# Two small transfers change queues: the weights go to GpSimd's, the last bottom rows to ScalarE's

## The chip, the cores and the metric

The kernel runs on one core of a Trainium2 chip. Time is device microseconds of one execution. The profile of an execution has a *span*, from its first to its last instruction. A run's time and its span are recorded separately. A run more than 1.5% above the fastest of its kernel is called slow, the others fast. All comparisons use fast runs. An engine's *stream* is the list of instructions that it runs.

## The reference

For eight images of 32 channels and 128 x 128 pixels: a group norm with 16 groups, a 3 x 3 convolution computed by FFT (whose crop places the valid outputs in one corner of each image), a bias, and the input added back.

```python
x = x + conv(group_norm(x, 16), weight, bias)     # (8, 32, 128, 128), float32
```

## The kernel before

The input is laid out with 128 partitions (four pixel phases x 32 channels), two images in each of four pairs. All 16.8 MB are loaded up front by SyncE, in order; every image is summed (VectorE), squared and summed (ScalarE), normalized (ScalarE), convolved as four matmuls per block of rows (PE), added back (VectorE); the rows and columns outside the convolution get the bias from GpSimd. Stores follow in order.

The loads; every DMA has a semaphore (a counter that tells when it has landed), and each issuing engine has its own queue (q1 is SyncE's, q10 ScalarE's, q0 GpSimd's):

```python
loaded[0] = []
for half in range(2):
    rows = slice(half * H // 2, (half + 1) * H // 2)
    loaded[0].append((rows.stop, load(xts[0][:, rows, :], x[0, :, 0, rows, :])))   # SyncE
    if half == 0:
        weights_in = load(wb_sb, wb, by="act")                                     # ScalarE
for img in range(1, 4):
    loaded[img] = [(H, load(xts[img], x[img // 2, :, img % 2]))]
# ... two more pairs of images
```

GpSimd prepares constants, then waits for the weights and spreads them out (twelve copies, four into `bias_sb` and eight into `w_sb`), then makes a tiny DMA of its own:

```python
w_zero = put("pool", lambda e: e.memset(w_sb, 0.0), mark=True)
# ... four times: bias_sb copy (waits for weights_in), two w_sb copies
warm_ok = keep_warm(0, 1, w_ok)        # a matmul on PE that waits for the last copy
# ...
turned = put("pool", lambda e: e.dma_start(turn, wb[0:6, ...]), adds="moved")
```

The end, for the last image:

```python
moved = store(most, last[0:MOST, :], biased[B - 1][0], turned, by="pool")         # 189 KB
store(to[:, N : H - REST, :], xt[:, N : H - REST, :], biased[B - 1][0])           # 800 KB
store(rest[MOST:P, :], last[MOST:P, :], biased[B - 1][0])                         # 3 KB
add(B - 1, 0, 2)
add(B - 1, 2, NCHUNK)
stored = store(to[:, 0:N, :], xt[:, 0:N, :], biased[B - 1][1], *added[B - 1])     # 1056 KB
```

## Time and profile before

| | before |
|---|---|
| time, median of the 6 runs beside the changed kernel | 83.23 us (83.12 to 83.44) |
| profiled run: time, span | 83.26 us, 82.03 us |
| so outside the span | 1.23 us |
| bytes moved | 33.62 MB |
| busy shares | PE 81%, VectorE 61%, ScalarE 58%, GpSimd 39%, DMA 97% |

The record of the changed kernel's runs, and of every run of the experiments, has the span, to 0.1 us, so the time outside it can be had to about 0.05 us. In all 42 runs of the kernel before, beside the experiments below, on three chips, it is 1.18 to 1.29 us, 1.24 on average.

The page's first lines also count instructions (the numbers behind the x). GpSimd's DMA issues are in its number, ScalarE's are not: the trace of part 1 alone, below, has one ScalarE instruction fewer than that of before (56 to 57), and both pages say x53. The counts in this document are those of the programs, and the traces agree with them.

```profile
span 82.0 us, 686 instructions
...
PE 66.8 (81%) x222; PEld 41.3 (50%) x222; DVE 50.2 (61%) x43; ACT 47.9 (58%) x53; POOL 31.6 (39%) x43
```

### The profile page before, as it was taken

The numbers are of one execution on the slowest core, as the hardware profiler recorded it, in microseconds if no ns is written. First come the engines' busy times: TensorE is split into PE (matmuls) and PEld (weight loads), VectorE is DVE, ScalarE is ACT, GpSimd is POOL, SyncE is SP. The second block draws the span as 40 slices with busy tenths as digits, with TensorE's granted clock in tenths as the row PEclk, the third lists the DMA queues.
The fourth block names the chain that finished last, engine by engine and source line by source line (L and its number), as shares of the span: only waits on it lengthen the run. The fifth ranks groups of instructions, "written<-read, shape, count | busy, mean of one in ns | idle before, by whom it ended". The sixth has DMA issues, their size and how long they took to land.

```text
span 82.0 us, 686 instructions
## 1 busy us (share of the span) xinstructions
PE 66.8 (81%) x222; PEld 41.3 (50%) x222; DVE 50.2 (61%) x43; ACT 47.9 (58%) x53; POOL 31.6 (39%) x43
## 2 busy tenths in 40 slices
PE   0009974999999999999999999999999999993000
PEld 0005433566666666666666656666666666660000
DVE  0009936960899499769949995996899324006000
ACT  3307967981699299569947974994798260000000
POOL 6876000004069900106992930490085029400000
PEclk9999998579999999999999999999999999999965
DMA  2899999999979979979959889989979999999995
GB/s 40 299 415 443 463 415 423 447 407 423 551 304 511 479 320 479 511 336 431 511 256 511 383 383 511 447 352 479 463 336 423 423 431 439 431 423 419 397 430 239
DMA packets 2164, 33.62 MB, mean 410 GB/s; under 512 B 296, under 2 KB 330, under 8 KB 500
## 3 DMA queue, kind: packets, MB, share of 16 engines
q1 hardware_dynamic: 2020, 33.36, 96.3%
q0 software_dynamic: 96, 0.19, 0.6%
q10 hardware_dynamic: 48, 0.06, 0.3%
HBM read 16.84 MB, written 16.78 MB: 410 GB/s over the span
## 4 chain that ended last, share of the span: by engine, by line
PE 74%; DMA 14%; DVE 2%; SPq 1%; issue 0%
PE ps L412 73%; DMA x<-x_dram 14%; DVE x L428 2%; PE ps_m L318 1%; SPq L183 1%; PE ps_w L265 0%
## 5 line engine op out<-in xcount | busy, mean ns | idle before, releaser
L412 PE MATMUL ps<-g,w_sb 128*128 128x363 f32 (+1 forms) x192 | 60.7, 473 | 0.1
L412 PEld LDWEIGHTS ps<-g,w_sb 128*128 128x128 f32 x192 | 36.1, 194 | 20.0 <-ACT origin L292 1.4
L283 DVE TENSOR_REDUCE sums<-x 128x1 f32<-128x4096 f32 x7 | 30.9, 4411 | 0.6 <-DMA x<-x_dram 0.6
L394 POOL TENSOR_SCALAR x<-x,bias_sb 128x1984 f32<-128x1984 f32 (+3 forms) x12 | 23.2, 1945 | 18.9 <-ACT origin L292 14.6
L303 ACT ACTIVATE unused<-x,origin 128x4096 f32<-128x4096 f32 (+1 forms) x9 | 30.0, 3330 | 0.3
L428 DVE SCALAR_TENSOR_TENSOR x<-ps,bias_sb,x 128x1089 f32<-128x1089 f32 (+2 forms) x9 | 10.9, 1220 | 7.7 <-PE ps L412 7.7
L373 ACT ACTIVATE g<-x,rstd 128x1089 f32<-128x1089 f32 (+2 forms) x8 | 9.4, 1190 | 3.4 <-DVE rstd L347 3.4
L283 DVE TENSOR_REDUCE first_sums<-x 128x1 f32<-128x2048 f32 x2 | 4.6, 2286 | 6.2 <-DMA x<-x_dram 6.2
L258 POOL COPY sums<-x 128x1 f32<-128x1 f32 x6 | 1.0, 186 | 18.2 <-DMA x<-x_dram 18.2
L335 DVE TENSOR_SCALAR var<-ps_m,square 128x1 f32<-128x1 f32 x8 | 1.8, 219 | 8.2 <-ACT square L330 8.2
L265 PE MATMUL ps_w<-x,avg 128*128 128x1 f32 x4 | 0.9, 304 | 7.1 <-POOL w_sb L476 6.1
L330 ACT ACTIVATE square<-ps_m,origin 128x1 f32<-128x1 f32 x8 | 2.1, 261 | 7.3 <-PE ps_m L318 7.3
L447 PE MATMUL ps<-x,avg 128*128 128x512 f32 x6 | 4.9, 942 | 0.0
L265 PEld LDWEIGHTS ps_w<-x,avg 128*128 128x128 f32 x4 | 0.8, 248 | 7.9 <-POOL w_sb L476 6.1
L318 PEld LDWEIGHTS ps_m<-sums,avg 128*128 128x128 f32 x16 | 2.8, 188 | 2.2 <-DVE x L428 1.0
L341 ACT ACTIVATE std<-var,eps 128x1 f32<-128x1 f32 x8 | 2.4, 294 | 2.3 <-DVE var L335 2.3
L344 DVE RECIPROCAL rstd<-std 128x1 f32<-128x1 f32 x8 | 1.3, 164 | 2.9 <-ACT std L341 2.9
L292 ACT ACTIVATE origin<-ps_w 128x1 f32<-128x1 f32 x2 | 0.3, 160 | 4.0 <-PE ps_w L265 4.0
L476 POOL COPY w_sb<-wb_sb 32x128 f32<-32x128 f32 (+1 forms) x8 | 2.5, 340 | 0.0
L318 PE MATMUL ps_m<-sums,avg 128*128 128x3 f32 x16 | 2.3, 214 | 0.0
L447 PEld LDWEIGHTS ps<-x,avg 128*128 128x128 f32 x6 | 1.5, 287 | 1.0 <-issue 1.0
L237 ACT ACT_TABLE_LOAD x1 | 1.3, 1283 | 1.2 <-PEq L579 1.2
(21 smaller groups left out, 13.3 us busy)
## 6 DMA issues: line engine op xcount, KB each, us to landing
x<-x_dram SPq DMA_DIRECT2D x2, 4096.0 KB, 34.3
out_dram<-x SPq DMA_DIRECT2D x2, 4096.0 KB
x<-x_dram SPq DMA_DIRECT2D x3, 2048.0 KB, 16.0
out_dram<-x SPq DMA_DIRECT2D x3, 2048.0 KB
x<-x_dram SPq DMA_DIRECT2D x2, 1024.0 KB, 6.2
out_dram<-x SPq DMA_DIRECT2D x1, 1056.0 KB
out_dram<-x SPq DMA_DIRECT2D x1, 800.0 KB
out_dram<-x POOLq DMA_DIRECT2D x1, 189.0 KB, 7.7
```

Of the source, the lines that this page charges most:

```text
L283: lambda e: e.tensor_reduce(to_sum(img, k)[:, 0:1], piece, mybir.AxisListType.X, ALU.add),
L303: lambda e: e.activation(unused[:, rows.start * W : rows.stop * W], piece, AF.Square, bias=origins[img], accum_out=to_sum(img, k)[:, 1:2],),
L318: lambda e: e.matmul(ps_ms[:, 0 : of.shape[1]], avg, of, start=(part == 0), stop=(part == last)),
L330: lambda e: e.activation(squares[img], ps_ms[:, 0:1], AF.Square, bias=origins[img]),
L335: lambda e: e.tensor_scalar(variances[img], ps_ms[:, 1:2], squares[img], None, op0=ALU.subtract),
L341: lambda e: e.activation(stds[img], variances[img], AF.Sqrt, bias=eps, scale=float(FFT * FFT)),
L373: lambda e: e.activation(g[:, rows, :], xt[:, LO + rows.start : LO + rows.stop, LO:W], AF.Identity, bias=rstd[:, 1:2], scale=rstd[:, 0:1],),
L394: put("pool", lambda e: e.tensor_scalar(part, part, 1.0, bias_sb, op0=ALU.mult, op1=ALU.add), *free, mark=mark)
L412: lambda e, k=k, dc=dc, rows=rows, top=top: e.matmul(ps[:, 0:rows, 0 : N - dc], w_sb[:, k * P : (k + 1) * P], g[:, top : top + rows, dc:N] ...
L428: lambda e: e.scalar_tensor_tensor(part, in0=ps, scalar=bias_sb, in1=part, op0=ALU.add, op1=ALU.add),
L447: "pe", lambda e: e.matmul(pss[1][:, 0, :], avg, piece, start=True, stop=True),
L476: lambda e: e.tensor_copy(w5[to, :, dc, :, c.start * C : c.stop * C], taps[:, 1 - rin : 5 - rin, b, :].rearrange("p (dr r) b o -> p dr r ( ...
```

## The change

Its apparent intent: take the weights off ScalarE at the start, and let the bottom rows of the last image leave beside image 6's store instead of behind it.

```diff
+    put.semaphore("moved")
+    weights_in = put("pool", lambda e: e.dma_start(wb_sb, wb), adds="moved")
     loaded[0] = []
     for half in range(2):
         ...
-        if half == 0:
-            weights_in = load(wb_sb, wb, by="act")
...
-    put.semaphore("moved")
...
-    store(to[:, N : H - REST, :], xt[:, N : H - REST, :], biased[B - 1][0])
+    store(to[:, N : H - REST, :], xt[:, N : H - REST, :], biased[B - 1][0], by="act")
```

## The prediction

> **What bounds the kernel now.** I read the chain of waits first, and distrusted it; then the DMA rows of the page, because 33.62 MB in 82 us is near what this core's engines can move.
>
> ```profile
> PE 74%; DMA 14%; DVE 2%; SPq 1%; issue 0%
> ...
> DMA  2899999999979979979959889989979999999995
> ...
> q1 hardware_dynamic: 2020, 33.36, 96.3%
> q0 software_dynamic: 96, 0.19, 0.6%
> q10 hardware_dynamic: 48, 0.06, 0.3%
> HBM read 16.84 MB, written 16.78 MB: 410 GB/s over the span
> ```
>
> The chain puts 74% on PE, but it stops at 76.1 us (the last add on DVE), six microseconds before the end. The queue shares add to 97.2% of the 16 engines' span: 79.7 us of 82.0. In the packet records of the trace the first packet starts at 1.84 us and the last ends at 81.62 us, 79.8 us in all. So there is hardly a moment without a packet on each engine. The table by stretches says the same with rates:
>
> ```profile
> 2.00:4.00 2.00, 0.00 (x0) 0.00 (x0) 0.00 (x0) 0.73 (x2) 1.84 (x4) 1.00 0.85 290
> 4.00:14.00 10.00, 6.29 (x15) 3.28 (x16) 5.81 (x6) 6.03 (x9) 3.01 (x13) 0.99 1.03 435
> ...
> 70.00:76.00 6.00, 4.54 (x17) 2.68 (x15) 1.42 (x2) 0.00 (x0) 0.72 (x2) 1.00 0.99 424
> 76.00:80.00 4.00, 0.00 (x0) 0.00 (x0) 0.06 (x1) 0.00 (x0) 0.00 (x0) 0.84 0.98 411
> 80.00:82.00 2.00, 0.00 (x0) 0.00 (x0) 0.00 (x0) 0.00 (x0) 0.00 (x0) 0.50 0.57 241
> ```
>
> The last two columns are the DMA share and GB/s: 0.96 or more in every stretch from 4 to 80 us, at 411 to 435 GB/s except around 41 us, where loads give way to stores (350 in 40:43). The stores queue behind one another all the way from there: the 4 MB store of the first pair is issued at 34.37 us and lands at 52.7, the next at 49.06 and lands at 62.4, then 56.41 to 67.4, 63.74 to 72.1, 68.58 to 77.6 (issue times and landings of the semaphores, from the trace). No store is issued late enough to leave the engines without work. The last one shows how much room is left:
>
> ```profile
> SPq L552 <- DMA out_dram<-x: 4.2, 1, 4.2
> ...
> 74.58 1.48 DVE x L428 x2
> ```
>
> DVE is done at 76.06; the last store (1056 KB) is issued at 76.09; its first packet starts only at 77.98, because packets of the bottom rows (800 KB, issued at 69.01) still run until 79.09. A DMA on free engines went from issue to first packet in 1.03 us (x, 0.81 to 1.84). So the last store could have come 77.98 - 76.09 - 1.03 = 0.86 us later without harm. PE, DVE and ACT have that much slack at the end; the bound is the total work of the 16 DMA engines.
>
> **What the Trainium skill says.**
> - "DMA: Bandwidth & Descriptors", section "Issuing engines are not separate DMA queues": DMAs issued by ScalarE, SyncE or GpSimd run on the same 16 engines and interleave, and several issuers save only sequencer time. The trace agrees: the weights' packets on q10 sit between x packets of q1, and while GpSimd's store runs (74.7 to 77.2 us) q1 slows by what q0 takes.
> - Same page, "Specifications": a fabric ceiling of 435 GB/s. The stretch 4:14 reads 435, so the stream is at it, and another queue can't raise it.
> - Same page, "Latency and other measured facts": first byte after about 600 ns on the hardware path, about 1 us on GpSimd's. Here the hardware path took 1.03 us, and GpSimd's two DMAs took 4.4 us (19.03 to 23.40) and 4.7 us (70.03 to 74.71), both with the engines full. The measurement decides: GpSimd's path is far slower than stated when q1 has a backlog.
> - Same page, "Why a DMA increments its semaphore by 16 and not by 1": how many engines share a DMA follows from the outer sizes, and a GpSimd DMA on fewer than 16 starts at a moving cursor. The weights have 32 rows, so 16 engines with two packets each: the trace has 32 packets of 1984 B. I expect that this leaves the cursor, and so the placing of GpSimd's store on 14 engines (42 packets of 4608 B in the trace), as it was; no run here shows it.
>
> **Part 1: the weights move from ScalarE's queue to GpSimd's.**
>
> ```profile
> 0.81 0.41 ACTq L183 DMA_DIRECT2D wb_sb<-wb_dram  x1
> ...
> 3.09 0.45 POOL L229 TENSOR_TENSOR avg<-half 128x128 f32<-128x128 f32 x1
> ...
> 4.46 0.18 POOL L472 COPY bias_sb<-wb_sb 32x1 f32<-32x1 f32 x1 [0.46 <-DMA wb_sb<-wb_dram]
> ...
> 7.00 0.63 POOL L476 COPY w_sb<-wb_sb 32x256 f32<-32x256 f32 x2
> ...
> 11.28 1.10 PE L447 MATMUL ps<-x,avg 128*128 128x512 f32 x2
> 13.39 0.38 PE L265 MATMUL ps_w<-x,avg 128*128 128x1 f32 x2 [1.00 <-DMA x<-x_dram]
> ```
>
> Removed: 0.41 us of issue on ScalarE, which has nothing to do then but its table load. Added: one issue ahead of GpSimd's chain. Its DMA at 19.03 took 0.74 us after 0.48 us of idle that the profile puts down to issue: about 1.2 us. That moves avg from 3.54 to about 4.8 us; the first matmul wants it when the first half image lands, at 5.97. Hidden, 1.2 us to spare.
>
> The landing: before, 4.41 us. After, the descriptors come at about 2 us, just as q1 fills. With the full 4.4 us to the first packet it would be 5.2, and then a second packet and a completion, each behind one x packet of 0.31 us (their duration at that stage), plus about 0.4 us to land: 6.7 us at worst. With less backlog, about 5. My estimate is 5.5, so 1.1 us later. The twelve copies from 4.46 to 7.63 us then end at about 8.7 (9.9 at worst). The first consumer on PE is the warming matmul at 11.28, and it can itself slip until 12.3 (13.39 less 1.10), as the next matmul waits for image 1, which lands at 13.34. So the slack is 3.6 to 4.7 us against 1.1 to 2.3 us of delay. Hidden as well.
>
> What DMA work changes? The same 32 packets of 81 ns (0.16 us per engine) and 16 completions go over another queue. Image 1's landing has the same bytes ahead of it either way. Net 0, perhaps a tenth either way in the ramp of the first two microseconds (290 GB/s).
>
> **Part 2: the bottom rows move from SyncE's queue to ScalarE's.** It removes one issue of 0.95 us from SyncE, which at that time has 5 us to wait for the last add anyway. ScalarE's last activation ends at 66.9 us, so it can issue at 69.0, as SyncE did. The 128 packets of 6400 B (0.244 us each, 8 per engine, 1.95 us per engine) no longer stand behind image 6's 2 MB but alternate with them: the bottom rows land earlier or at the same time, image 6 later, both finished by about 79.1 as before, since each engine has the same packets to do. The last store stays on q1, and its 8 packets of 0.319 us per engine follow: 79.1 + 2.55 gives 81.6, and 0.34 us to land gives 81.96, as now. When two queues mixed in the trace (76.5 to 77.0), the packets' summed rate was 417 instead of 431 GB/s: over six microseconds 14/431 would be 0.2 us, but those packets were smaller, so I count 0 to 0.1 us.
>
> **Sum:** 0 (GpSimd's issue) + 0 (weights later) + 0 to 0.1 (mixing) - 0 to 0.1 (a freer ramp, SyncE free earlier) = 0 on 83.19 us. I put it at 83.15.
>
> **The rivals.**
> - *The weights become the bound at the start.* For it: GpSimd's DMAs took 6.6 and 7.7 us from issue to landing. Against it: even a landing at 8.5 us ends the copies at 11.7, before 12.3, and then the end has 0.86 us more slack. The time moves only by what exceeds about 10.0 us of landing. If that comes: 83.5 to 84.
> - *Two queues fill the engines better.* For it: the ramp and the tail (80:82 at 0.57) are not full, and the engines' last landings spread from 80.86 to 81.96. Against it: 411 to 435 GB/s everywhere else, and each engine's sum of packets stays. If it holds: 82.7 to 82.9.
> - *The placing of GpSimd's store turns.* A cursor moved by the weights would put its 13.8 KB per engine (three packets of 0.178 us, 0.53 us) on other engines; if the last one gets them: 83.5. If a late one loses them: 82.9.
>
> **Range and chances.** Runs of one kernel spread by 0.14 us (83.12 to 83.26); the rivals reach 0.3 to 0.4 us to either side. So 82.8 to 83.5. A change of 2% is 1.66 us; nothing above comes near it: 0.01 faster, 0.98 same, 0.01 slower.
>
> **What would show it.** Right: the DMA shares still add to about 97%, with first packet at 1.8 and last end near 81.6; GpSimd's first copy starts at 5 to 6.7 us; image 1's matmul still waits for its landing at about 13.3; bottom rows' packets lie among image 6's, which lands near 79; the last landing is near 82. Wrong: the warming matmul waiting for the weight copies past 12.3 us, a DMA row with a gap before the last store, or last landings of the engines spread by much more than 1.1 us.

## The result and the profile after

The changed kernel took 83.96 us (median of 6 runs, 83.46 to 84.08), the kernel before 83.23. A ratio here is the mean time of one kernel's fast runs over that of the other's fast runs of the same rounds, so it isn't quite the ratio of the medians: 1.0076, 95% interval 1.0048 to 1.0104. It is slower by 0.6 to 0.7 us, well inside the 2% within which two times count as the same here, but outside the predicted range (82.8 to 83.5).

The span does not show where. First the page of the changed kernel:

```profile
span 82.0 us, 686 instructions
...
PE 67.0 (82%) x222; PEld 41.2 (50%) x222; DVE 50.2 (61%) x43; ACT 48.0 (59%) x53; POOL 32.1 (39%) x44
...
DMA  2899999998979979959969889989979999999995
...
q1 hardware_dynamic: 1876, 32.54, 94.0%
q10 hardware_dynamic: 144, 0.82, 2.4%
q0 software_dynamic: 128, 0.26, 0.8%
```

The span is 82.0 us, as before; the queue shares still add to 97.2%. The table by stretches (its last two columns: DMA share, GB/s) differs from that of before, in these two columns and from 4 us on, by 6% at most:

```profile
4.00:14.00 10.00, 7.42 (x15) 3.75 (x15) 5.75 (x6) 6.01 (x9) 4.20 (x15) 1.00 1.04 430
...
70.00:76.00 6.00, 3.61 (x14) 2.11 (x12) 1.48 (x2) 0.00 (x0) 0.00 (x0) 1.00 1.00 427
76.00:80.00 4.00, 0.00 (x0) 0.00 (x0) 0.00 (x0) 0.00 (x0) 0.00 (x0) 0.59 1.01 425
80.00:82.00 2.00, 0.00 (x0) 0.00 (x0) 0.00 (x0) 0.00 (x0) 0.00 (x0) 0.50 0.54 228
```

At the start, the timeline shows the weights going the slow way and still coming in time:

```profile
1.36 0.71 POOL L186 DMA_DIRECT2D wb_sb<-wb_dram  x1 [0.85 <-POOLq L578]
...
4.37 0.45 POOL L229 TENSOR_TENSOR avg<-half 128x128 f32<-128x128 f32 x1
...
7.09 0.18 POOL L471 COPY bias_sb<-wb_sb 32x1 f32<-32x1 f32 x1 [1.81 <-DMA wb_sb<-wb_dram]
...
9.63 0.63 POOL L475 COPY w_sb<-wb_sb 32x256 f32<-32x256 f32 x2
...
11.38 2.05 PE L446 MATMUL ps<-x,avg 128*128 128x512 f32 x2
13.45 0.50 PEld L265 LDWEIGHTS ps_w<-x,avg 128*128 128x128 f32 x2 [1.59 <-DMA x<-x_dram]
```

The copies end at 10.26 us, the matmul that wants them starts at 11.38, and PE's next weight load then still waits for image 1. At the end:

```profile
68.08 0.37 ACTq L436 DMA_DIRECT2D out_dram<-x  x1
...
73.65 1.48 DVE L428 SCALAR_TENSOR_TENSOR x<-ps,bias_sb,x 128x726 f32<-128x726 f32 x2 [6.04 <-PE ps L412]
```

By the landings in the trace, the bottom rows and image 6 are both in by 79.6 us and the last store at 81.95, against 81.96 before. One thing happened by itself that supports the bound: PE's and VectorE's chain ran 0.9 us earlier in this run (VectorE's last add ends at 75.13 instead of 76.06, the last store is issued at 75.16 instead of 76.09), and the end did not move.

So where are the 0.7 us? The six runs' times less their spans are 1.92, 1.95, 1.90, 1.46, 1.68 and 1.80 us, 1.78 on average, against the 1.24 of the kernel before. Of the difference of the means (83.88 - 83.25 = 0.64 us) 0.55 us lie outside the span. The records of the trace go on beyond the span, and the view of DMA queues, asked for the stretch from 82 to 84 us, has one packet there. After:

```profile
DMA  0000000000000000000000000000000000600000
...
DMA packets 1, 0.01 MB, mean 4 GB/s; under 512 B 0, under 2 KB 0, under 8 KB 0
...
q14 instruction: 1, 0.01, 1.7%
```

The same view of the kernel before, over 82 to 85 us:

```profile
DMA packets 0, 0.00 MB, mean 0 GB/s; under 512 B 0, under 2 KB 0, under 8 KB 0
```

q14 is the queue that carries instructions. In the packet records the one after is 8192 bytes, from 83.70 to 84.23 us, 1.69 us after the end of the span. Everything else after the end takes as long in both: the updates of semaphore 2, which come one after another, lie 0.12 to 0.29 us after the span; the resets of all semaphores 0.25 to 0.85; a second round on semaphore 2 1.08 to 1.44. The packet comes after that.

Two cautions. The counted time does not simply begin with the span's first instruction: in the kernel before, the second round ends 1.44 us after the span, and 1.23 us were counted outside it; after, the packet ends 2.2 us after the span, and 1.9 were counted. So "outside the span" is not shown to be "behind its end". But the start is no better place: in all seventeen traces the updates of semaphore 2 in the last 0.37 us before the first instruction lie alike, and the group before these begins 3.11 us before it both in the changed kernel (1.9 us outside) and in its version with sixteen memsets more, below (1.2 us). And the results are not late: the last store landed as before.

### The profile page after: what moved, and what is told of

It reads as the page before. It is cut to its first block, busy times and chain, and to the rows that moved or that the text cites. A ratio compares the mean times of both kernels' runs of the same rounds, so it can differ in the third digit from the quotient of the medians.

```text
span 82.0 us, 686 instructions
## 1 busy us (share of the span) xinstructions
PE 67.0 (82%) x222; PEld 41.2 (50%) x222; DVE 50.2 (61%) x43; ACT 48.0 (59%) x53; POOL 32.1 (39%) x44
## 4 chain that ended last, share of the span: by engine, by line
PE 76%; DMA 9%; DVE 5%; SPq 0%; issue 0%
PE ps L412 71%; DMA x<-x_dram 9%; DVE first_sums L283 3%; PE ps L446 2%; PE ps_m L318 2%; DVE x L428 2%; PE ps_w L265 1%; SPq L183 0%
## 5 line engine op out<-in xcount | busy, mean ns | idle before, releaser
L412 PE MATMUL ps<-g,w_sb 128*128 128x363 f32 (+1 forms) x192 | 59.7, 467 | 0.0
L412 PEld LDWEIGHTS ps<-g,w_sb 128*128 128x128 f32 x192 | 35.5, 191 | 19.4 <-ACT origin L292 1.4
L446 PE MATMUL ps<-x,avg 128*128 128x512 f32 x6 | 5.8, 1108 | 0.0
L318 PEld LDWEIGHTS ps_m<-first_sums,avg 128*128 128x128 f32 x4 | 1.2, 323 | 2.0 <-ACT unused L303 1.5
```

Source lines behind the costliest of these rows:

```text
L318: lambda e: e.matmul(ps_ms[:, 0 : of.shape[1]], avg, of, start=(part == 0), stop=(part == last)),
L412: lambda e, k=k, dc=dc, rows=rows, top=top: e.matmul(ps[:, 0:rows, 0 : N - dc], w_sb[:, k * P : (k + 1) * P], g[:, top : top + rows, dc:N] ...
L446: "pe", lambda e: e.matmul(pss[1][:, 0, :], avg, piece, start=True, stop=True),
```

## The experiments

Fifteen kernels, all correct, each timed in five rounds against the kernel before on the same chip. The first question was whether the cost belongs to a DMA at all, or to the length of an engine's stream of instructions.

### Part 1 alone

```diff
 (the changed kernel)
-    store(to[:, N : H - REST, :], ..., biased[B - 1][0], by="act")
+    store(to[:, N : H - REST, :], ..., biased[B - 1][0])
```

> The changed kernel's span from first to last instruction is 82.0 us, as before, yet its time is 83.96 against 83.23 us: 0.7 us lie after the last instruction, where its trace has an 8 KB packet of instructions from 83.70 to 84.24 us that the trace of before lacks. This run has part 1 alone (weights on GpSimd's queue, bottom rows on SyncE's). Theory F (GpSimd's stream is one instruction longer, and that makes one more instruction fetch at the end): time 83.9 to 84.0, span 82.0, the late 8 KB packet there. Theory G (a software DMA at the start costs time outside the span): the same time, so this run does not tell F from G. Theory H (ScalarE's late store costs time at the end): 83.2 and no late packet.

Measured: 83.43 us against 83.43, ratio 0.9991 (0.9943 to 1.0040); in these rounds the kernel before spread from 83.09 to 84.33, so the time outside the span says more: 1.43 to 1.50 us, against 1.19 to 1.29. No late packet. That is neither the number of F and G nor H's: a cost of 0.2 us, not 0.6.

### Part 2 alone

```diff
 (the kernel before)
-    store(to[:, N : H - REST, :], ..., biased[B - 1][0])
+    store(to[:, N : H - REST, :], ..., biased[B - 1][0], by="act")
```

> Part 2 alone (weights on ScalarE's queue, bottom rows stored by ScalarE). ScalarE then has one instruction more than in either kernel, SyncE one fewer, GpSimd as before. Theories F and G: 83.2, span 82.0, no packet of instructions after the end. Theory H: 83.9 to 84.0, with the late packet.

Measured: 83.69 us median with two slow runs in it; ratio of the fast runs 1.0007 (0.9941 to 1.0072). Outside the span, fast runs: 1.28 to 1.37 us. No late packet. The 1.88 that later expectations mention was one of the slow runs. Theory H falls: the late store on ScalarE costs about 0.1 us, not 0.7.

### One memset more on GpSimd, no DMA moved

```diff
 (the kernel before)
     eps_ok = put("pool", lambda e: e.memset(eps, ...), mark=True)
+    spare = sbuf("spare", P, 1)
+    put("pool", lambda e: e.memset(spare, 0.0))
```

> The kernel before with one tiny memset more on GpSimd (128x1, to a tile that nobody reads), so GpSimd's stream is as long as in the changed kernel and no DMA moves. Theory F: 83.9 to 84.0 with an unchanged span of 82.0 and a late 8 KB packet. Theories G and H: 83.2, none.

Measured: 84.03 us; ratio 1.005 (0.9996 to 1.0104, in the same restless rounds). The span is 82.1, outside it 1.79 to 1.97 us in the fast runs (the 1.67 quoted later was a slow run), and the trace has an 8 KB packet of instructions from 83.86 us, 1.71 us after the span (the view from 82 to 85 us):

```profile
DMA packets 1, 0.01 MB, mean 3 GB/s; under 512 B 0, under 2 KB 0, under 8 KB 0
...
q14 instruction: 1, 0.01, 1.1%
```

A memset that takes a tenth of a microsecond, where GpSimd has time to spare, costs the whole price of the change. Theory G, that the software DMA is what costs, is not needed.

### The changed kernel with one memset fewer on GpSimd

```diff
 (the changed kernel)
-    eps_ok = put("pool", lambda e: e.memset(eps, ...), mark=True)
+    eps_ok = put("dve", lambda e: e.memset(eps, ...), mark=True)
```

> The changed kernel with the memset of eps moved from GpSimd to VectorE, so GpSimd's stream is as long as before; all DMAs as in the changed kernel. Theory F: back to 83.2, no late packet. Theories G and H: 83.9 to 84.0.

Measured: 83.23 us, ratio 0.9966 (0.9917 to 1.0014); outside 1.22 to 1.29 us; no late packet. All DMAs are those of the changed kernel, VectorE has one instruction more, and the cost is gone: Theory G falls.

### Sixteen memsets more, before and changed

```diff
+    spare = sbuf("spare", P, 16)
+    for k in range(16):
+        put("pool", lambda e: e.memset(spare[:, k : k + 1], 0.0))     # at 19 us, GpSimd idles there
     sum_squares(1)
```

> So far the time outside the span (time of a run less its span) is 1.19 to 1.29 us for before, 1.46 to 1.95 changed, 1.43 to 1.50 with part 1 alone, 1.28 to 1.37 (once 1.88) with part 2 alone, 1.67 to 1.97 with one memset more on GpSimd, 1.22 to 1.29 for the changed kernel with one memset fewer. This run: before with 16 memsets (128x1) more on GpSimd, at 19 us where it idles. Theory F1 (GpSimd's stream crosses a block of instructions just at its end, after the kernel's last instruction; a longer stream crosses earlier, where the fetch is hidden): outside 1.2 to 1.5, time 83.2 to 83.5, and no late packet. Theory F2 (any stream longer than a limit pays): outside 1.9, time 83.9.

> The changed kernel with 16 memsets (128x1) more on GpSimd at 19 us, where it idles. Theory F1: a longer stream is faster, outside 1.2 to 1.5, time 83.2 to 83.5, span 82.0. Theory F2: outside 1.9, time 83.9.

Measured, before with sixteen more: ratio 1.0006 (0.9982 to 1.0030), outside 1.21 to 1.27 us. Changed with sixteen more: 83.22 us, ratio to before 0.9997 (0.9974 to 1.0019), outside 1.21 to 1.28. This is the sharpest result: the changed kernel gets 0.7 us *faster* by sixteen useless instructions (not in the same rounds, but each against the kernel before: 1.0076 and 0.9997). Its page counts them, and its queue list has a row that neither original has:

```profile
PE 68.3 (83%) x222; PEld 42.0 (51%) x222; DVE 50.2 (61%) x43; ACT 47.9 (58%) x53; POOL 32.7 (40%) x60
...
q14 instruction: 1, 0.01, 0.0%
```

The packet of instructions now lies inside the span, at 63.99 us (62.80 in the other), while GpSimd waits for its next piece of work. Theory F2 (any longer stream pays) falls; F1 stands. I call a length at which a stream costs time, while a longer one does not, its *edge*.

### Four and two memsets more

> Before with 4 memsets more on GpSimd at 19 us. One more paid 0.6 us outside the span with an 8 KB packet of instructions 1.7 us after it; sixteen more paid nothing (outside 1.21 to 1.27), with the packet at 62.8 us inside the kernel. If the packet's place moves smoothly with the length: some of the cost, outside 1.3 to 1.9, packet near the end. If only the very edge of a block pays: outside 1.2 to 1.3, packet inside the kernel, after 63 us.

> Before with 2 memsets more on GpSimd at 19 us. One more cost 0.6 us outside the span, four more 0.05, sixteen more none. If the edge is one instruction wide: outside 1.2 to 1.35, time 83.3. If it is wider: 1.5 to 1.9, time 83.6 to 83.9.

The same edit of the kernel before with 4 and 2 in place of 16. Four: outside 1.24 to 1.33 us, ratio 1.0007 (0.9993 to 1.0021), no packet of instructions after the kernel's start. Two: outside 1.60 to 1.89, 83.90 us, ratio 1.0067 (1.0042 to 1.0091). So the costly edge is at least two instructions wide and gone at four. "Packet inside the kernel" was wrong for four: there is none. And in the profiled run with two (outside 1.60, the lowest of its six) there is no late packet either, so a visible packet and the cost don't go together in every run.

### ScalarE's stream

```diff
     put("act", lambda e: e.activation(warm, eps, AF.Sqrt), eps_ok)
+    put("act", lambda e: e.activation(spare, eps, AF.Identity), eps_ok)      # once, or 16 times
```

> Part 1 alone had GpSimd +1 and ScalarE -1 instructions and paid only 0.2 us; the changed kernel has GpSimd +1 and ScalarE as before and paid 0.6. This run is part 1 with one tiny activation more on ScalarE: GpSimd +1, ScalarE as before, SyncE as before. If ScalarE's count matters beside GpSimd's: outside 1.8 to 1.95 with the late packet, time 83.9. If GpSimd's alone counts, or the bottom store itself matters: 1.43 to 1.50, time 83.4.

> Before with one tiny activation more on ScalarE, no DMA moved. If ScalarE's count alone costs: outside 1.4 or more. If it costs only together with GpSimd's extra instruction: 1.2 to 1.35, as with part 2 alone.

> Before with 16 tiny activations more on ScalarE between 2.5 and 6 us, where it idles. One more gave 1.28 to 1.75 outside, two of six at 1.75. If ScalarE's stream has such an edge as GpSimd's: outside back at 1.2 to 1.3, with an 8 KB packet inside the kernel. If more instructions on ScalarE cost by themselves: 1.4 or more. The span may move by some tenths as the activations delay the first squares; only the time outside it is asked.

Part 1 with one activation more: 83.63 us, ratio 1.0052 (1.0027 to 1.0076), outside 1.55 to 1.85, no late packet in the profiled run (again the lowest of its runs). That lies between the two answers expected, nearer the first: ScalarE's count matters beside GpSimd's. Before with one more: ratio 1.0041 (1.0013 to 1.0070), outside 1.28 to 1.38 in four runs and 1.74 to 1.75 in two: both answers came, run by run. (The slow run of part 2 alone with 1.88 looks like these two; there too ScalarE's stream is one longer.) Before with sixteen more: 1.0010 (0.9996 to 1.0024), outside 1.19 to 1.27, with a packet of instructions at 40.51 us. ScalarE's stream has such an edge too, and a longer stream avoids it likewise.

### Weights on SyncE's queue, and part 1 with sixteen memsets

```diff
-        weights_in = load(wb_sb, wb, by="act")
+        weights_in = load(wb_sb, wb)                  # SyncE, between the halves of image 0
```

> Before with the weights loaded by SyncE between the two halves of image 0: ScalarE one instruction fewer, GpSimd as before, SyncE one more. If only a stream just past its edge pays: outside 1.2 to 1.3 and time as before, 83.2. If ScalarE's missing instruction is what put part 1 alone at 1.45: 1.4 or more.

> Part 1 alone (outside 1.43 to 1.50) with 16 memsets more on GpSimd at 19 us. If those 0.2 us are the edge of GpSimd's stream too: outside 1.2 to 1.3, packet near 63 us, time 83.2. If a software DMA at the start costs them: still 1.43 to 1.50.

Weights by SyncE (ScalarE one instruction fewer): ratio 1.0024 (1.0011 to 1.0038), outside 1.34 to 1.41. In the trace (of the slowest of its six runs, 84.54 us), the last two updates of the second round on semaphore 2 come at 1.50 and 1.55 us after the span instead of 1.39 and 1.44, 0.11 us later. Part 1 with sixteen memsets more on GpSimd (ScalarE one fewer): outside 1.36 to 1.40, the same late pair (1.50 and 1.54), the packet at 62.40 us. So of part 1's 0.2 us, about 0.13 belong to ScalarE's missing instruction and under 0.1 to GpSimd's extra one.

### GpSimd at its edge, ScalarE away from it

> Before with 1 memset more on GpSimd (alone: outside 1.67 to 1.97) and 16 activations more on ScalarE (alone: 1.19 to 1.27). If GpSimd's edge pays alone: 1.67 to 1.97, time 83.9. If it pays only while ScalarE's stream ends at its own edge too: 1.2 to 1.4, time 83.3.

> The changed kernel with 16 activations more on ScalarE between 2.5 and 6 us. If GpSimd's edge pays alone: outside 1.5 to 1.95 as changed, time 83.9. If only together with ScalarE's: 1.2 to 1.4, time 83.3.

The edits are those above, together. Before with one memset and sixteen activations more: outside 1.42 to 1.54 us, ratio 1.0044 (1.0014 to 1.0074). The changed kernel with sixteen activations more: outside 1.45 to 1.48, ratio 1.0021 (0.9996 to 1.0046). Both fall between what the two answers expected. GpSimd's edge costs 0.23 to 0.25 us with ScalarE's stream sixteen longer (mean 1.49 and 1.47 against 1.24); with ScalarE's stream at its length of before it costs 0.5 to 0.7 on average (changed, one memset, two memsets, part 1 with one activation).

The round on semaphore 2 tells two kinds of cost apart. The small ones are seen there, as late updates: 0.11 us where ScalarE's stream is one shorter (three kernels), 0.08 where it is one longer (part 2 alone and one activation), 0.05 with four memsets. The large one is not: in the changed kernel, with one and two memsets, and with one GpSimd instruction more beside one or sixteen activations, the round ends 1.43 to 1.44 us after the span, as before, though 1.48 to 1.93 us were counted outside it in the same runs.

Together (counts against the kernel before; time outside the span in fast runs; instructions' 8 KB packet after the start, in the profiled run):

| kernel | GpSimd | ScalarE | outside, us | packet at, us |
|---|---|---|---|---|
| before | 0 | 0 | 1.18 to 1.29 | none |
| changed | +1 | 0 | 1.46 to 1.95 | 83.70 |
| one memset more | +1 | 0 | 1.79 to 1.97 | 83.86 |
| two memsets more | +2 | 0 | 1.60 to 1.89 | none |
| four more | +4 | 0 | 1.24 to 1.33 | none |
| sixteen more | +16 | 0 | 1.21 to 1.27 | 62.80 |
| changed, sixteen more | +17 | 0 | 1.21 to 1.28 | 63.99 |
| changed, eps by VectorE | 0 | 0 | 1.22 to 1.29 | none |
| part 1 alone | +1 | -1 | 1.43 to 1.50 | none |
| part 1, one activation more | +1 | 0 | 1.55 to 1.85 | none |
| part 2 alone | 0 | +1 | 1.28 to 1.37 | none |
| before, one activation more | 0 | +1 | 1.28 to 1.75 | none |
| before, 16 activations | 0 | +16 | 1.19 to 1.27 | 40.51 |
| weights by SyncE | 0 | -1 | 1.34 to 1.41 | none |
| part 1, 16 memsets | +17 | -1 | 1.36 to 1.40 | 62.40 |
| before, one memset and 16 activations | +1 | +16 | 1.42 to 1.54 | 39.42 |
| changed, 16 activations | +1 | +16 | 1.45 to 1.48 | 42.36 |

No kernel beats the kernel before clearly. The changed kernel with sixteen memsets, or with eps set by VectorE, is not told apart from it.

## Why the prediction was wrong

**The bound: right.** DMA stayed at 97.2% of 16 engines' span, the span did not change, and the run itself supplied a test, though the DMAs had changed too: a chain of PE and VectorE 0.9 us earlier changed nothing at the end.

**GpSimd's issue: right.** avg was to come at about 4.8 us; it came at 4.82 (4.37 + 0.45).

**The weights' landing: mechanism right, size too small.** I had 5.5 us, 6.7 at worst; it was 7.04. The term mis-sized is the start: I counted the 4.4 us to the first packet from 0.81 us, but the DMA instruction began at 1.36; its first packet came 4.1 us later, at 5.47. (The worst case's own items, 5.2 + 2 x 0.31 + 0.16 + 0.4, add up to 6.4, not to 6.7.) The copies ended at 10.26 us instead of the 9.9 of the worst case; the slack until 12.3 held. The 32 packets of 81 ns became 16 packets of 3968 bytes and 154 ns, the same work.

**The bottom rows: right.** They and image 6 finished together by 79.6 us (the packets themselves at 79.1, as expected), the last store landed at 81.95. Mixing cost less than I allowed: between 72 and 78 us the packets' summed rate was 427 to 430 GB/s, against 431 at 70 us.

**The sum: this is the step that failed.** "Sum: 0 (GpSimd's issue) + 0 (weights later) + 0 to 0.1 (mixing) - 0 to 0.1 ... = 0 on 83.19 us" adds changes of the span to a time that is 1.2 us longer than the span. The 1.2 us were taken for a constant, and they are not: they went from 1.24 to 1.78 on average. All three rivals lay inside the span too, and so did the signs of being wrong, of which none came: no copy held a matmul past 12.3 us, and the last landings spread from 80.97 to 81.95 us (before: 80.86 to 81.96). That 83.96 lies in the first rival's "83.5 to 84" is chance; its mechanism did not occur. The missing term is one instruction more on GpSimd: +0.55 us outside the span.

**What is shown of the cause, and what is open.** Shown: the cost follows the length of the instruction streams, not the DMAs. One memset without any DMA moved brings it, one fewer removes it with all DMAs moved, sixteen more remove it as well. What GpSimd's extra instruction costs depends on ScalarE's stream: 0.5 to 0.7 us on average with it as before, about 0.25 with it sixteen longer, under 0.1 with it one shorter (which by itself costs 0.13). Argued from the place of the packets, not shown: that the time is a wait for a block of instructions which the end of the stream just spills into, and which a longer stream fetches in the middle of the kernel, where nobody waits. The Trainium skill, "Runtime: NRT & Kernel Launch", section "Instruction fetch mechanics", describes such blocks, fetched ahead while the current one runs, and calls the cost of crossing one "mostly hidden"; the packets at 40 and 63 us agree with that; the one at 83.7 us would be the exception, if it is such a block. The same page's section "The ~15µs preamble/postamble breakdown" lists a barrier, resets of 51 semaphores per engine and another barrier after the kernel; the trace agrees in that order, with five groups of 46 to 51 neighbouring semaphores in the two traces. Open: why the two streams act together; why the profiled runs with 1.5 to 1.6 us outside show no late packet while the two with 1.9 do; why four memsets more have neither the cost nor a packet inside the kernel; and whether the lengths themselves matter, or where the streams come to lie in memory.

## What to carry to other kernels

Subtract the span from the time before predicting, and after: if a small change moves the time and leaves the span, look outside it, not at the queues. Where a few tenths matter, count each engine's instructions, in the program as well as on the page, which left out ScalarE's DMA issues, and try a variant with a few more or fewer on the engine that changed, before blaming the operation that was moved. This kernel, bound by its 16 DMA engines, gained nothing in its span (82.0 us both times) from having two transfers spread over other queues.

## What the Trainium skill lacked or had wrong

- "Runtime: NRT & Kernel Launch", "Instruction fetch mechanics": the crossing of a block is called mostly hidden. If the late packet is such a crossing, which is argued and not shown, it was not hidden at the end of a stream: 1.24 to 1.78 us outside the span for one instruction more. The packets here are 8192 bytes; the page speaks of 16 KiB blocks, and whether a packet is a whole block is not shown.
- The same page, "The ~15µs preamble/postamble breakdown": resets of the semaphores are given 1.5 us; in these traces they run from 0.25 to 0.85 us after the span, 0.6 us.
- "DMA: Bandwidth & Descriptors", "Latency and other measured facts": first byte on GpSimd's path about 1 us. With SyncE's queue in use it was 4.1 to 4.8 us from issue to first packet, in all five GpSimd DMAs of the two profiles.
- No page says that a kernel's time can fall when instructions are added: 83.96 to 83.22 us with sixteen memsets (ratios to the kernel before: 1.0076 and 0.9997).
